# Memory and place of the turned even tiles between a first attention and a long convolution

## The chip, the cores and the metric

The kernel runs on one core of one Trainium2 chip. The metric is the device time of one execution in microseconds (us), the median of several runs. In the profile PE is TensorE, DVE is VectorE, ACT is ScalarE, POOL is GpSimd, and SP is SyncE, whose queue (SPq) issues nearly all transfers. An engine executes its instructions in the order in which they stand in its queue; an instruction that waits holds everything behind it on that engine.

## The reference

Two decoder layers are applied to a token matrix of 8 batches of 256 tokens with 512 features, in float32. After each of the six parts the result is added to the input and layer-normed.

```python
x = _layernorm(x + _L0_attn_ref(x, ...))            # differential attention, causal
x = _layernorm(x + _L0_xattn_ref(x, k, fside, ctx_2048, ctx_2048, 8))   # long convolution
x = _layernorm(x + _L0_ffn_ref(x, ...))             # 8 experts, two for each token
x = _layernorm(x + _L1_attn_ref(x, ...))            # causal attention
x = _layernorm(x + _L1_xattn_ref(x, ..., ctx_2048, ctx_2048, ...))      # cross attention
x = _layernorm(x + _L1_ffn_ref(x, ...))             # causal attention, one shared head by token
```

This case is about the border between the first two. The convolution takes the attended tokens and the context, forms their products kv for each group of 8 channels, filters kv along the features with a filter from `k`, and multiplies by the context again:

```python
kv = vr[:, :, :, None, :] * x2r[:, :, None, :, :]
y = irfft(rfft(kv, n=1024) * rfft(k, n=1024))[..., :512]
out = einsum('bhijl,bhil->bhjl', y + kv * skip, x1r)
```

Here the token position is the channel and the features are the axis that is filtered, so both inputs are needed turned: features on partitions, tokens on the free axis.

## The kernel before, in words

**Tiles.** The tokens lie in 16 tiles `x[t]` of 128 tokens by 512 features (NT = 16; t even is the first half of a batch, t odd the second). A turned tile is made by four PE transposes into PSUM and one copy out: `turned` (L227, copy on ACT at L232) inside an attention, `transpose` (L167, PE at L171) elsewhere, whose `evacuate` alternates the copy between ACT (L121) and DVE (L123).

**The first attention** (`diff_attention`, L291, through `causal_attention`, L1225) runs 64 units, 8 for each batch, in an order that is written out by hand for PE, DVE, ACT and POOL. A unit makes scores for row maxima (`maxima`, L1287), and nine units later the scores again as weights (`weights`: PE L1350 and L1359, exponential on ACT L1367, causal mask on POOL L1368) and the products with the values and with ones (`products`: PE L1393 and L1403, reciprocal on DVE L1411). Side work is put between these steps by `fill`, which spends a budget on each unit: first the steps of a list `after`, in order of the unit for which they were entered by `at(slots, "fill", ...)`, then a queue with due units. Side work of the last units: the output products (`ps_o`, PE L207), sums of squares and their powers (PE L514, L527, L553 with POOL L543 for the last batch but one; PE L450, L465 with POOL L458 and ACT L459 for the last batch, where each pair of units is scaled by itself), residuals and norms (DVE L267, L150, L151, L160, POOL L145, L146).

**The context.** From unit 54 on, one context tile is turned each unit (`turn_context`, PE L231, ACT L232) into a small buffer `cT`, and stored turned in DRAM as `ctx_d` (SP L429); it is loaded two tiles ahead (`load_context`, SP L424).

**The convolution** (`long_conv`, L571) works on two halves, i = 0 for the even tiles and i = 1 for the odd ones. `xh[i]` are turned tokens and `ch[i]` the turned context of a half. It loads `ch[0]` and `ch[1]` from `ctx_d` (SP L587), turns the even tiles into `xh[0]`, and then runs 32 groups h, the first 16 on half 0. A group loads its filter tile `wt` (SP L601, three buffers), makes kv on DVE and POOL (L607), side products u on POOL (L615, L616) with a sum `us` on DVE (L623), runs ten matmuls `ps_y` (PE L177, each two records in the trace) and multiplies and sums their results on DVE (L642, L645). The odd tiles are written down inside groups 0 and 1, and group 2 issues the loads of the experts' weights `gu` (SP L714, three of 2,816 KB). Their order on each engine is decided by the scheduler.

**Memory.** The four turned halves lie in two tiles of 32 KB a partition: `first` (`first_h`) holds `xh[0]` and `ch[0]`, `w` (`w_l1a`) holds `xh[1]` and `ch[1]`. In the built program `w` lies at bytes 196,576 to 229,344 of a partition, which nothing of the first attention uses, and `first` at 163,808 to 196,576, over the attention's buffers for residuals, wide rows, context and `cT` (its work memory ends at 196,256). A tile that is put over older ones waits for their last use. Later `w` takes the weights of the second layer's self attention; `first` takes the last part of the experts' weights, and after it is given back, `w_x` (`w_l1x`, a tile of the same size, elsewhere) takes the experts' gathered rows (`combine`, L1193) and the weights of the cross attention.

Of the kernel before, what the change touches and what calls it, by code (L numbers as in the profile page):

```python
# [17 lines left out]
F32 = mybir.dt.float32  # L18
# [6 lines left out]
P = 128  # L25
B, S, D = 8, 256, 512
NT = B * S // P
# [3 lines left out]
KB = D // P  # L31
# [14 lines left out]
PH = NT // 2  # L46
NE = (PH * 2 * P - E * (P - 1) - 1) // P + 1
VB = 64
NV = (NT - TPG) * P // VB + H1


@with_exitstack
def decoder_kernel(ctx: ExitStack, tc: tile.TileContext, a: dict, out: bass.AP):
    nc = tc.nc
    xin = a["x"].rearrange("b s d -> (b s) d").rearrange("(t p) d -> p t d", p=P)
    cin = a["ctx_2048"].rearrange("b s d -> (b s) d").rearrange("(t p) d -> p t d", p=P)
# [9 lines left out]
    x = []  # L66
# [134 lines left out]
    MM, TR = 0.86, 0.45  # L201
# [25 lines left out]
    def turned(pools, dst, src, tag="mm"):  # L227

        pt = pools.tile([P, KB, P], F32, tag=tag, name="pt")
        for k in range(KB):  # L230
            nc.tensor.transpose(pt[:, k, :], src[:, k * P : (k + 1) * P], ident)  # L231
        nc.scalar.copy(dst, pt)  # L232
# [55 lines left out]

    def diff_attention():  # L291

# [5 lines left out]
        w = wpool.tile([P, 7168], F32, tag="w", name="w_l0")  # L298
# [5 lines left out]
        for t in range(4):  # L304
            nc.sync.dma_start(
                out=wo[32 * t : 32 * t + 32],
                in_=a["L0_attn_Wo"][P * t : P * (t + 1), :].rearrange("(k d) c -> d k c", d=32),
# [5 lines left out]
        for i, n in enumerate(("q1", "k1", "q2", "k2")):  # L313
            nc.sync.dma_start(
                out=lv[:, i, :],
                in_=a[f"L0_attn_lambda_{n}"].unsqueeze(0).broadcast_to([P, HD0]),
# [13 lines left out]
        half = const.tile([P, 2], F32, tag="half", name="half")  # L330
# [25 lines left out]
        def prepare(work, pools, g, at, here):  # L356
            qT = work.tile([P, KB, GT], F32, tag="qT", name="qT")
            kz = work.tile([P, 2, GT], F32, tag="kz", name="kz")
            v = work.tile([P, TPG, P], F32, tag="v", name="v", bufs=3)
            xT, turns = turned_group(work, pools, g)  # L360
            batches = [slice(b * S, (b + 1) * S) for b in range(2)]

            def values(ti, ps=[]):
                if ti == 0:
                    ps.append(pools.tile([P, TPG, P], F32, tag="mm", name="ps_v"))
                for k in range(KB):
                    by_columns(
                        ps[-1][:, ti, :],
                        xT[0][:, k, ti * P : (ti + 1) * P],
                        wv[:, k, :],  # L370
                        k == 0,
                        k == KB - 1,
                    )
# [18 lines left out]

            if g:

                need = turns + [(0, values_steps), (0, keys(slice(0, GT)))]
            else:
                need = turns[:2] + [(0, keys(batches[0]))]
                need += [(3, steps) for _, steps in turns[2:]]
                need += [(8, keys(batches[1])), (9, values_steps)]
            for b, tokens in enumerate(batches):  # L400
                for c, first in enumerate((0, 1, 4, 5)):
                    block = feature_block(pools, qT, xT, wq, 0, c, HD0**-0.5, tokens)
                    need.append((8 * b + first, block))
            need.sort(key=lambda piece: piece[0])

            if g == NG - 1:

                for t in range(2):
                    load_context(work, t)
                for t in range(NT):  # L410
                    slot = 16 * g + 6 + t
                    at(slot - here, "fill", [(TR, lambda t=t: turn_context(work, pools, t))])
            return (
                need,
                lambda rows, c, at, n: qT[rows, c // 4 * 2 + c % 2, at : at + n],
                lambda rows, c, at, n: kz[rows, c // 2 % 2, at : at + n],
                lambda k, h: v[:, k, 32 * (h % 4) : 32 * (h % 4) + 32],
            )

        cx = {}  # L420

        def load_context(work, t):
            cx[t] = work.tile([P, D], F32, tag="cx", name="cx")
            nc.sync.dma_start(out=cx[t], in_=cin[:, t, :])  # L424

        def turn_context(work, pools, t):
            c = work.tile([P, KB, P], F32, tag="cT", name="cT")
            turned(pools, c, cx.pop(t))
            nc.sync.dma_start(out=ctx_d[:, :, t * P : (t + 1) * P], in_=c)  # L429
            if t + 2 < NT:  # L430
                load_context(work, t + 2)

        def gather(work, pools, at, yT, n, c, o, r):

# [136 lines left out]
    def long_conv(router, load_experts, xh, ch, ps_t, meanwhile):  # L571
# [5 lines left out]
        with ExitStack() as st:  # L577
# [4 lines left out]
            sk = work.tile([P, S], F32, tag="skip", name="skip", bufs=1)  # L582
            nc.sync.dma_start(out=sk, in_=skip.unsqueeze(0).broadcast_to([P, S]))
            tokens = ctx_d.rearrange("p k (b i s) -> p k b i s", b=B, i=2)
            for i in range(2):
                for k in range(KB):
                    nc.sync.dma_start(out=ch[i][:, k], in_=tokens[:, k, :, i, :])  # L587

            def turn(t):
                transpose(ps_t, xh[t % 2][:, :, t // 2, :], x[t])  # L590

            for t in range(0, NT, 2):
                turn(t)
            route = router(work)
            shape = [P, B, NHEAD, NHEAD]
            for h in range(NH):
                i, at = divmod(h * NHEAD, P)
# [979 lines left out]
    def self_weights(w, behind):  # L1577
        return load_w(w, 0, a["L1_attn_w_qkv"], 3 * D, behind), load_w(
            w, 3 * D * KB, a["L1_attn_w_o"], D, behind
        )  # L1580

    def self_attention(wqkv, wo, arrive):


# [76 lines left out]
    def cross_weights(w):  # L1661
        return [
            load_w(w, i * D * KB, a[f"L1_xattn_{n}"], D)
            for i, n in enumerate(("wq", "wk", "wv", "wo"))
        ]
# [519 lines left out]
        causal_attention("r", prepare, finish)  # L2185

    masks, clear_slots, load_experts, load_gu_last, router, blocks, combine, wide = experts(rt)
    diff_attention()
    with ExitStack() as st_self:


        half = B * P * KB
        pool = st_self.enter_context(
            tc.tile_pool(name="w_self", bufs=1, side="right", reuse_waits="tile")
        )
        w = pool.tile([P, 2 * half], F32, tag="w", name="w_l1a")
        with ExitStack() as st_blocks:
            pool = st_blocks.enter_context(
                tc.tile_pool(name="c_half", bufs=1, side="right", reuse_waits="tile")
            )  # L2200
            first = pool.tile([P, 2 * half], F32, tag="first", name="first_h")
            ps_t = st_blocks.enter_context(tc.tile_pool(name="c_pst", bufs=2, space=PSUM))
            parts = [
                [m[:, i * half : (i + 1) * half].rearrange("p (k b s) -> p k b s", k=KB, b=B) for m in (first, w)]
                for i in range(2)
            ]
            ends = [first[:, i * half : (i + 1) * half] for i in range(2)]
            late_tokens = long_conv(
                lambda work: router(work, w[:, half:]),
                load_experts,  # L2210
                parts[0],
                parts[1],
                ps_t,
                lambda: load_gu_last(ends),
            )
            w_self = []
            blocks(
                ps_t,
                [m[:, E * FF + i * D : E * FF + (i + 1) * D] for m in ends for i in range(2)],
                late_tokens,  # L2220
                lambda behind: w_self.extend(self_weights(w, behind)),
            )
        wide.close()
        x[:] = x_tiles(ctx.enter_context(tc.tile_pool(name="xb", bufs=1)))
        st_cross = ExitStack()
        pool = st_cross.enter_context(tc.tile_pool(name="w_cross", bufs=1))
        w_x = pool.tile([P, 8192], F32, tag="w", name="w_l1x")
        w_cross = []

        def arrive(t):  # L2230
            load, add, norm = combine(t, w_x)

            def last():
                norm()
                if t == NT - 1:
                    w_cross.extend(cross_weights(w_x))

            return load, add, last

        self_attention(*w_self, arrive)  # L2240
    with tc.tile_pool(name="w_routed", bufs=1, side="right") as pool:
        w_routed = routed_weights(pool.tile([P, 6400], F32, tag="w", name="w_l1f"))
        cross_attention(*w_cross)
        st_cross.close()
        routed_attention(*w_routed)
# [55 lines left out]
```

## Time and profile before

| | |
|---|---|
| time, median of 3 runs | 2091.62 us (2087.61 to 2092.78) |
| the profiled execution: its time and its span | 2084.03 us, 2082.3 us |
| what lies around the span | 1.7 us |
| mean granted clock of TensorE | 0.979 |
| busy: PE, DVE, POOL, ACT | 1926.0, 1236.9, 851.9, 615.3 us |
| last norm of the first attention (DVE L160, starts) | 465.57 us |
| first convolution matmul (`ps_y`, starts) | 476.4 us |
| last convolution matmul (starts) | 774.0 us |

The span is one execution from the first instruction to the last, and all positions below are in us from its start. The profiled execution was 7.6 us faster than the median of the runs, so its durations are used for differences, and a difference is then added to the median. PE's busy time counts modelled ends of pipelined matmuls. Rows of the timeline merge instructions of one line that follow each other; "idle before" names what the engine waited for.

### The profile page before, as it was taken

The numbers are of one execution on the slowest core, as the hardware profiler recorded it, in microseconds if no ns is written. First come the engines' busy times: TensorE is split into PE (matmuls) and PEld (weight loads), VectorE is DVE, ScalarE is ACT, GpSimd is POOL, SyncE is SP. The second block draws the span as 40 slices with busy tenths as digits, with TensorE's granted clock in tenths as the row PEclk, the third lists the DMA queues.
The fourth block names the chain that finished last, engine by engine and source line by source line (L and its number), as shares of the span: only waits on it lengthen the run. The fifth ranks groups of instructions, "written<-read, shape, count | busy, mean of one in ns | idle before, by whom it ended". The sixth has DMA issues, their size and how long they took to land. (4 is left out here: it accounts for less than half of the span.)

```text
span 2082.3 us, 46237 instructions
## 1 busy us (share of the span) xinstructions
PE 1926.0 (92%) x20068; PEld 1122.6 (54%) x20068; DVE 1236.9 (59%) x1879; ACT 615.3 (30%) x787; POOL 851.9 (41%) x945
## 2 busy tenths in 40 slices
PE   7979999879999999999969999998999999988985
PEld 5545555444444446666635545544878778454443
DVE  4677777658889876122225657457343442536887
ACT  4555555520000003211114344431101011235552
POOL 2677777646555834000014545344000000216763
PEclk9999999989999999999989999999999999999997
DMA  6799943326114217223122202002000000170000
GB/s 220 307 399 387 386 139 78 88 69 224 44 58 140 80 51 233 85 72 138 61 86 83 78 31 89 3 2 103 21 21 31 21 31 1 43 233 12 30 24 31
DMA packets 141627, 220.27 MB, mean 106 GB/s; under 512 B 27440, under 2 KB 56240, under 8 KB 141424
## 3 DMA queue, kind: packets, MB, share of 16 engines
q1 hardware_dynamic: 134960, 196.97, 27.5%
q0 software_dynamic: 6464, 20.32, 2.9%
q8 instruction: 160, 2.62, 0.5%
q14 instruction: 43, 0.35, 0.1%
HBM read 106.51 MB, written 123.34 MB: 110 GB/s over the span
## 5 line engine op out<-in xcount | busy, mean ns | idle before, releaser
L1411 DVE RECIPROCAL rsum<-ps_pv 128x256 f32<-128x256 f32 x128 | 224.5, 1754 | 220.2 <-PE ps_pv L1403 220.2
L177 PE MATMUL ps_y<-kv,wt 128*128 128x512 f32 x640 | 280.2, 597 | 5.4 <-POOL kv L607 2.7
L1367 ACT ACTIVATE pT<-ps_k 128x1536 f32<-128x1536 f32 x128 | 185.7, 1451 | 239.1 <-PE ps_k L1359 233.5
L1307 DVE TENSOR_REDUCE neg<-rows 128x12 f32<-128x1536 f32 x128 | 222.9, 1742 | 48.2 <-POOL rows L1298 48.1
L1296 ACT COPY rows<-ps_q 128x1536 f32<-128x1536 f32 x128 | 184.1, 1438 | 154.2 <-PE ps_q L1287 101.1
L1368 POOL TENSOR_SCALAR_AFFINE_SELECT pT<-pT 128x1024 f32<-128x1024 f32 x128 | 140.7, 1100 | 186.2 <-ACT pT L1367 186.1
L177 PEld LDWEIGHTS ps_y<-kv,wt 128*128 128x128 f32 x640 | 120.9, 191 | 156.7 <-issue 137.4
L1298 POOL TENSOR_SCALAR_AFFINE_SELECT rows<-rows 128x1024 f32<-128x1024 f32 x128 | 141.2, 1103 | 154.0 <-ACT rows L1296 153.4
L1378 POOL TENSOR_TENSOR pT<-pT 128x512 f32<-128x512 f32 x112 | 147.1, 1313 | 9.3
L1204 POOL DMA_INDIRECT w_l1x<-ys,slots x32 | 33.5, 1046 | 258.5 <-DMA ys<-y_m 250.9
L207 PE MATMUL ps_f<-xT,w_l1a 128*32 128x256 f32 x2048 | 122.0, 384 | 0.7 <-ACT xT L232 0.7
L145 POOL TENSOR_SCALAR rstd<-bn_mv 128x1 f32<-128x1 f32 x80 | 16.6, 207 | 206.8 <-DVE bn_mv L151 200.5
L1112 PE MATMUL po_m<-dn,hT 128*128 (+1 forms) x216 | 98.7, 594 | 1.0 <-ACT hT L1102 1.0
L1403 PE MATMUL ps_pv<-pT,ones_v 128*32 128x256 f32 (+1 forms) x1152 | 85.2, 378 | 14.7 <-POOL pT L1378 14.6
L645 DVE TENSOR_REDUCE yc<-z 128x64 f32<-128x512 f32 x128 | 86.2, 674 | 5.6 <-POOL w_l1a L646 5.2
L207 PEld LDWEIGHTS ps_f<-xT,w_l1a 128*32 128x32 f32 x2048 | 62.2, 111 | 45.3 <-issue 7.3
L1287 PE MATMUL ps_q<-kz,qT 32*128 32x128 f32 x1536 | 62.2, 292 | 16.8 <-ACT pT L1367 13.4
L1287 PEld LDWEIGHTS ps_q<-kT,qT 32*128 32x128 f32 x1536 | 48.7, 186 | 50.4 <-ACT pT L1367 17.3
L1350 PE MATMUL ps_k<-qT,kT 32*128 32x256 f32 (+1 forms) x1024 | 69.8, 359 | 5.1 <-ACT rows L1296 2.9
L1287 PEld LDWEIGHTS ps_q<-kz,qT 32*128 32x128 f32 x1536 | 49.8, 190 | 45.4 <-ACT pT L1367 31.8
L1091 DVE TENSOR_TENSOR h_b<-h_b,pg 128x352 f32<-128x352 f32 x36 | 18.8, 521 | 92.4 <-ACT h_b L1090 92.4
L1287 PE MATMUL ps_q<-kT,qT 32*128 32x128 f32 x1536 | 61.0, 288 | 13.4 <-ACT pT L1367 8.5
(385 smaller groups left out, 3617.4 us busy)
## 6 DMA issues: line engine op xcount, KB each, us to landing
xs<-zero SPq DMA_DIRECT2D x8, 4352.0 KB, 32.5
ys<-zero SPq DMA_DIRECT2D x8, 4352.0 KB, 33.1
filters<-in_L_xattn_k SPq DMA_DIRECT2D x4, 2560.0 KB
first_h<-xs SPq DMA_DIRECT2D x36, 256.0 KB, 2.7
ys<-y_m SPq DMA_DIRECT2D x36, 256.0 KB, 2.0
gu<-in_L_ffn_gate_up_proj SPq DMA_DIRECT2D x3, 2816.0 KB, 16.4
wt<-filters SPq DMA_DIRECT2D x32, 256.0 KB, 2.6
sorted_x<-zero SPq DMA_DIRECT2D x1, 5120.0 KB, 34.7
```

The lines of the kernel that those rows point to most:

```text
L177: nc.tensor.matmul(ps, lhsT=lhsT(k), rhs=rhs(k), start=(k == 0), stop=(k == n - 1))
L207: nc.tensor.matmul(ps[cs], lhsT=lhsT[:, cs], rhs=rhs, start=start, stop=stop)
L645: nc.vector.tensor_reduce(yc[:, lb], z, AX.X, ALU.add)
L1112: nc.tensor.matmul(po, lhsT=hT[:m, i, :], rhs=dn[i][:m, bass.ds(e, 1), :], start=(i == 0), stop=(i == len(FCH) - 1),)
L1287: nc.tensor.matmul(block[:, s, j, :], lhsT=q(rows, c, b * S + i * P, P), rhs=k(rows, c, b * S + keys * P, P), start=True, stop=True,)
L1296: nc.scalar.copy(d.rearrange("p j s k -> p s j k"), block)
L1298: nc.gpsimd.affine_select(out=rows, in_=rows, compare_op=ALU.is_ge, fill=-FAR, base=0, pattern=[[0, 8], [-1, P]], channel_multiplier=1,)
L1307: return lambda: nc.vector.tensor_reduce(neg[u // upb % 2][:, :, :, c], d, AX.X, ALU.max, negate=True)
L1367: nc.scalar.activation(p[:, 0:3].rearrange("p j s q -> p s j q"), block, AF.Exp)
L1368: nc.gpsimd.affine_select(out=p[:, 0:2].rearrange("p j s q -> p (j s) q"), in_=p[:, 0:2].rearrange("p j s q -> p (j s) q"), compare_op=ALU ...
L1378: nc.gpsimd.tensor_tensor(p[:, 3], p[:, 1], p[:, 2], ALU.add)
L1411: nc.vector.reciprocal(r, ps[:, 1, :])
```

## The change

`first` is now allocated before the first attention, at the outer end of the right side of the memory, and kept until the cross attention is done. In the built program it lies where `w` was (196,576 to 229,344), and `w` now lies over the attention's buffers (163,808 to 196,576). `diff_attention` gets the two halves of `first`:

- Context tiles are taken in the order 0, 2, ..., 14, 1, 3, ..., 15. The even ones are turned directly into `ch[0]`, and stored from there; the odd ones go through `cT` as before. So `long_conv` loads `ch[1]` alone.
- Six steps `turn_first` (EARLY = 6) turn the tiles x[0], x[2], ..., x[10] into `xh[0]`, entered at units 62 to 67. `long_conv` turns only x[12] and x[14] of the even tiles.
- `first` also takes the place of `w_x`, and the weights of the last part go to the left side of the memory.

In the built program the instructions of the attention's last units are ordered anew, since six steps more pass through `fill`. At the start of the convolution PE has the remaining turns, all eight odd ones included, and the four small matmuls `ps_cs` of the routing ahead of the first `ps_y`; SP has `skip`, the four loads of `ch[1]`, three filter tiles, the three loads of `gu`, and then the other filter tiles (before: `ch[1]`, `skip`, `ch[0]`, five filter tiles, `gu`). After that the order on every engine is the old one, but for a memset that moves by two instructions.

```diff
+EARLY = B - 2
-    def diff_attention():
+    def diff_attention(xh, ch):
...
-                for t in range(NT):
-                    slot = 16 * g + 6 + t
-                    at(slot - here, "fill", [(TR, lambda t=t: turn_context(work, pools, t))])
+                for i in range(NT):
+                    slot = 16 * g + 6 + i
+                    at(slot - here, "fill", [(TR, lambda i=i: turn_context(work, pools, i))])
+                for b in range(EARLY):
+
+                    def turn_first(b=b):
+                        turned(pools, xh[:, :, b, :], x[2 * b])
+
+                    at(16 * g + 14 + b - here, "fill", [(TR, turn_first)])
...
+        order = [*range(0, NT, 2), *range(1, NT, 2)]
...
-        def turn_context(work, pools, t):
-            c = work.tile([P, KB, P], F32, tag="cT", name="cT")
-            turned(pools, c, cx.pop(t))
+        def turn_context(work, pools, i):
+            t = order[i]
+            if t % 2:
+                c = work.tile([P, KB, P], F32, tag="cT", name="cT")
+            else:
+                c = ch[:, :, t // 2, :]
+            turned(pools, c, cx.pop(i))
             nc.sync.dma_start(out=ctx_d[:, :, t * P : (t + 1) * P], in_=c)
...
-            for i in range(2):
-                for k in range(KB):
-                    nc.sync.dma_start(out=ch[i][:, k], in_=tokens[:, k, :, i, :])
+            for k in range(KB):
+                nc.sync.dma_start(out=ch[1][:, k], in_=tokens[:, k, :, 1, :])
...
-            for t in range(0, NT, 2):
+            for t in range(2 * EARLY, NT, 2):
                 turn(t)
...
-    diff_attention()
+    st_cross = ExitStack()
+    pool = st_cross.enter_context(tc.tile_pool(name="w_first", bufs=1, side="right"))
+    first = pool.tile([P, 2 * half], F32, tag="first", name="first_h")
...
+    diff_attention(in_batches(first, 0), in_batches(first, 1))
...
-            pool = st_blocks.enter_context(
-                tc.tile_pool(name="c_half", bufs=1, side="right", reuse_waits="tile")
-            )
-            first = pool.tile([P, 2 * half], F32, tag="first", name="first_h")
...
-        st_cross = ExitStack()
-        pool = st_cross.enter_context(tc.tile_pool(name="w_cross", bufs=1))
-        w_x = pool.tile([P, 8192], F32, tag="w", name="w_l1x")
...
-            load, add, norm = combine(t, w_x)
+            load, add, norm = combine(t, first)
...
-    with tc.tile_pool(name="w_routed", bufs=1, side="right") as pool:
+    with tc.tile_pool(name="w_routed", bufs=1) as pool:
```

More of the change, by code (lines that the diff above doesn't have):

```diff
@@ L406, in prepare @@
             if g == NG - 1:
-                for t in range(2):
-                    load_context(work, t)
-                for t in range(NT):
-                    slot = 16 * g + 6 + t
-                    at(slot - here, "fill", [(TR, lambda t=t: turn_context(work, pools, t))])
+                for i in range(2):
+                    load_context(work, i)
+                for i in range(NT):
[5 more added lines that the diff above has]
+                    at(16 * g + 14 + b - here, "fill", [(TR, turn_first)])
             return (
@@ L420, in diff_attention, with load_context @@
         cx = {}
-        def load_context(work, t):
-            cx[t] = work.tile([P, D], F32, tag="cx", name="cx")
-            nc.sync.dma_start(out=cx[t], in_=cin[:, t, :])
-        def turn_context(work, pools, t):
-            c = work.tile([P, KB, P], F32, tag="cT", name="cT")
-            turned(pools, c, cx.pop(t))
+        order = [*range(0, NT, 2), *range(1, NT, 2)]
+        def load_context(work, i):
+            cx[i] = work.tile([P, D], F32, tag="cx", name="cx")
+            nc.sync.dma_start(out=cx[i], in_=cin[:, order[i], :])
+        def turn_context(work, pools, i):
[5 more added lines that the diff above has]
+            turned(pools, c, cx.pop(i))
             nc.sync.dma_start(out=ctx_d[:, :, t * P : (t + 1) * P], in_=c)
-            if t + 2 < NT:
-                load_context(work, t + 2)
+            if i + 2 < NT:
+                load_context(work, i + 2)
         def gather(work, pools, at, yT, n, c, o, r):
@@ L2187, in decoder_kernel, with in_batches @@
     masks, clear_slots, load_experts, load_gu_last, router, blocks, combine, wide = experts(rt)
-    diff_attention()
+    half = B * P * KB
+    st_cross = ExitStack()
+    pool = st_cross.enter_context(tc.tile_pool(name="w_first", bufs=1, side="right"))
+    first = pool.tile([P, 2 * half], F32, tag="first", name="first_h")
+    def in_batches(m, i):
+        return m[:, i * half : (i + 1) * half].rearrange("p (k b s) -> p k b s", k=KB, b=B)
+    diff_attention(in_batches(first, 0), in_batches(first, 1))
     with ExitStack() as st_self:
-        half = B * P * KB
         pool = st_self.enter_context(
@@ L2197, in decoder_kernel @@
         with ExitStack() as st_blocks:
-            pool = st_blocks.enter_context(
-                tc.tile_pool(name="c_half", bufs=1, side="right", reuse_waits="tile")
-            )
-            first = pool.tile([P, 2 * half], F32, tag="first", name="first_h")
             ps_t = st_blocks.enter_context(tc.tile_pool(name="c_pst", bufs=2, space=PSUM))
[L2203 to L2206, printed above, removed]
+            parts = [[in_batches(m, i) for m in (first, w)] for i in range(2)]
             ends = [first[:, i * half : (i + 1) * half] for i in range(2)]
@@ L2235, in last @@
                 if t == NT - 1:
-                    w_cross.extend(cross_weights(w_x))
+                    w_cross.extend(cross_weights(first))
             return load, add, last
         self_attention(*w_self, arrive)
-    with tc.tile_pool(name="w_routed", bufs=1, side="right") as pool:
+    with tc.tile_pool(name="w_routed", bufs=1) as pool:
         w_routed = routed_weights(pool.tile([P, 6400], F32, tag="w", name="w_l1f"))
```

## The prediction

> **What bounds the kernel now.** First the page's busy times:
>
> ```profile
> PE 1926.0 (92%) x20068; PEld 1122.6 (54%) x20068; DVE 1236.9 (59%) x1879; ACT 615.3 (30%) x787; POOL 851.9 (41%) x945
> ```
>
> PE is the bound on average, so the places that matter are those where it idles. I looked at the border between attention and convolution, first in the timeline of PE (start, us, engine, line, operation, records; in brackets the idle time before and what ended it):
>
> ```profile
> 424.79 0.86 PE L1393 MATMUL ps_pv<-pT,v 128*32 128x256 f32 x16 [2.03 <-POOL pT L1368]
> ...
> 445.31 0.86 PE L1393 MATMUL ps_pv<-pT,v 128*32 128x256 f32 x16 [0.49 <-DVE res L267]
> ...
> 449.12 0.44 PE L465 MATMUL pt_rr<-ident,wide 128*128 128x128 f32 x2 [2.31 <-ACT wide L459]
> 449.49 5.36 PE L207 MATMUL ps_o<-w_l,yT_b 128*32 128x512 f32 x48
> ...
> 459.07 3.64 PE L207 MATMUL ps_o<-w_l,yT_b 128*32 128x512 f32 x16 [0.58 <-DVE yT_b L468]
> 466.91 5.86 PE L171 MATMUL pt<-ident,x 128*128 128x128 f32 x28 [4.20 <-ACT first_h L121]
> ...
> 476.44 4.13 PE L177 MATMUL ps_y<-kv,wt 128*128 128x512 f32 x9 [0.19 <-DMA wt<-filters]
> ```
>
> The last products start at 445.31; 4.20 us of idle stand before the turns, and `ps_y` starts at 476.44, released by a filter tile. The timeline of SP's queue says why that tile comes so late:
>
> ```profile
> 430.19 3.88 SPq L587 DMA_DIRECT2D w_l1a<-ctx_d  x4
> 440.84 0.35 SPq L583 DMA_DIRECT2D skip<-in_fside_S  x1
> 466.27 3.68 SPq L587 DMA_DIRECT2D first_h<-ctx_d  x4
> 470.00 24.22 SPq L601 DMA_DIRECT2D wt<-filters  x5
> 498.13 6.86 SPq L714 DMA_DIRECT2D gu<-in_L_ffn_gate_up_proj  x3
> ```
>
> The odd context (`w_l1a`) goes out at 430.19, during the attention. The even one waits until 466.27, and the filters stand behind it. In the timeline of DVE, what it waits for is the last norm of `x[15]`, whose input `res` lies under `first`; it ends at 465.57 + 0.55 = 466.12:
>
> ```profile
> 465.57 0.55 DVE L160 TENSOR_SCALAR x<-res,bn_mv,rstd 128x512 f32<-128x512 f32 x1 [0.72 <-POOL rstd L146]
> ```
>
> The border thus has four stretches: up to the last products, from there to the norm (445.31 to 466.12, 20.8 us), from the norm to the first `ps_y` (10.3 us), and the first groups.
>
> **The change part by part.** The profiled execution takes 2084.03 us (span 2082.3 and 1.7 around it); the median is 2091.62. Differences are made against the former and added to the latter.
>
> *Memory and queue.* `first` becomes free early, but `w` takes its place over `res`. The loads of `ch[1]`, 2 MB like those of `ch[0]`, now wait for the norm of `x[15]`, and they still stand ahead of the filters on SP. So the transfers from norm to first filter tile are the old ones: four context loads, then `wt`, 10.2 us. What the change takes off this path (loading `ch[0]`) it puts back as `ch[1]`.
>
> *A, last units of the attention.* Six turns enter. One turn costs PE 0.58, 0.49 and 0.58 us (from the start of an L231 row to the next row: 417.24 to 417.82, 426.23 to 426.72, 409.64 to 410.22): 6 × 0.55 = 3.3. Behind the last products move two of the turns L171 (1.04 together at 443.78), one L450 (0.47) and one L465 (0.25): −1.8. Net +1.5. The six copies on ACT (0.58 each) are hidden: ACT is busy some 6 to 14 us of 52 here, and nothing of PE waits for them soon; uncovered they would cost 3.5.
>
> The order also makes a new wait. In one late unit POOL now has, between two masks L1368, two L543 and one L458; PE's L465, which needs that L458 by way of ACT, stands ahead of the next unit's scores, and behind it are those scores, the weights and the products of the unit. The timeline of POOL has the prices:
>
> ```profile
> 420.43 3.26 POOL L543 TENSOR_TENSOR rr<-rr,neg_half 128x8 f32<-128x8 f32 x2
> 423.64 1.09 POOL L1368 TENSOR_SCALAR_AFFINE_SELECT pT<-pT 128x1024 f32<-128x1024 f32 x1
> 424.70 1.64 POOL L458 TENSOR_TENSOR rr<-rr,neg_half 128x8 f32<-128x8 f32 x1
> ```
>
> 3.26 + 1.64 = 4.9 us, of which one product step of PE (about 1.5, L1393 and L1403) lies beside: +3.4. Against it, waits of PE before (5.6 us between 403 and 445, among them the 2.03 shown at 424.79, and 1.97 at 412.83) partly go, since the turns fill them: −2. A = 1.5 + 3.4 − 2 = +3. Bounds: no new wait, and all that the turns can fill goes (1.5 − 3.3 = −1.8); the whole wait and nothing filled (+4.9). I take +3: the order fixes the new wait, and of the old ones I let one of about 2 us be filled.
>
> *B, last products to last norm.* The moved L450, L465 and the order of the `ps_o` blocks (24, 8 of the last batch's tiles) lengthen the steps before the 48 records, which I place 7.5 us after the products instead of 4.2; the wait of 2.42 us for ACT `wide` that stood later goes. Added up by the rows: 7.5 + 5.4 (48 records) + 0.8 (L465 and its DVE step) + 1.9 (16 records, by their row of 1.90 at 431.82) + 3.4 (462.71 to 466.12) = 19.1. Before, 20.8 with the last 16 records at 3.64 us instead of 1.90: the same 19.1 at full clock. Whether these records meet the half clock decides: −1.7 to +1.7, and I take 0.
>
> *C, norm to first `ps_y`, 10.3 before.* The filter comes at 10.2 as before. The other chain: one copy of `x[14]`'s turn 0.7, kv and u on POOL (1.06 + 1.17 + 1.06 + 0.72 + 0.72 = 4.7), `us` 0.4, two copies of odd turns 1.3 and three kv 2.2 on DVE, `us` 0.4, copy 0.7, the turn of `x[15]` 0.7 and the four `ps_cs` 0.95, which PE now has ahead of `ps_y`: 12.05. Being later, it decides: +1.7 (bounds −0.1, if the filter alone decides, to +3.3, if DVE's kv and POOL's do not overlap as well).
>
> *D, first groups.* Before, 100 records of `ps_y` take from 476.44 to 523.64, 47.2 us; at 0.438 each (five groups of 20 records, 8.76 each) they are 43.8. The 3.4 us are three odd turns, `ps_cs` and a wait of 1.84 us at 497.45, all of which now lie ahead of the first `ps_y`: −3.4 (bound 0, if `ps_y` waits for kv instead).
>
> *E, the clock.* Windows of 3.41 us (busy us and instructions of each engine, then granted clock, DMA share, GB/s):
>
> ```profile
> 457.47:460.88 3.41, 2.50 (x14) 0.78 (x18) 0.42 (x1) 0.28 (x1) 0.00 (x0) 0.50 0.00 0
> 460.88:464.29 3.41, 1.83 (x12) 0.10 (x4) 3.01 (x6) 0.00 (x0) 0.74 (x2) 0.50 0.00 0
> 464.29:467.70 3.41, 0.79 (x4) 0.79 (x5) 1.80 (x4) 0.58 (x1) 0.94 (x2) 0.50 0.06 11
> 467.70:471.12 3.42, 3.42 (x17) 2.84 (x16) 0.99 (x2) 1.17 (x2) 0.00 (x0) 0.50 1.12 299
> 471.12:474.53 3.41, 2.64 (x19) 1.76 (x17) 2.57 (x5) 1.56 (x3) 0.00 (x0) 1.00 1.19 291
> ```
>
> After a thin window those that follow run at half clock, and a full window brings the clock back. Now about nine turns (5 us of work) are spread over the 12 us to `ps_y`, 41% busy, so that the first 3.4 us of `ps_y` may run at half: one window's work done by half, +1.7 (0 to +3.4).
>
> The Trainium skill ("TensorE: Matmul & The Clock Gate", Part 4) speaks against such a stretch: it says that PE's transposes are not counted as busy and do not bring the full clock. The rows differ: from 467.70 to 471.12 PE had turns alone, and 1.00 follows. By the rule the first window of `ps_y` is at half clock whatever the turns' density; by the row only if they are sparse.
>
> *Later stages.* The orders are the old ones. The even context is no longer loaded, and the loads of odd context move where they were. The cross attention's context is ready some 30 us before it is used; its new waits hide there. I cost them at nothing; uncovered, one wait shifts by 3 us at most.
>
> *Sum.* 3 + 0 + 1.7 − 3.4 + 1.7 = +3.0: 2087.0 us for an execution like the profiled one, 2094.6 for the median. A measurement can tell 0.3%, 6.3 us, from no change.
>
> **The rivals.** *(1) The forecast: next to nothing, −3 to +6.* A load is exchanged for a load, and six turns of PE work change place.
>
> *(2) Faster.* If the norm no longer gates the filter (SP past the context sooner), or the even group's kv is ready at once, `ps_y` starts 7 us earlier: with A at its lower end and D, 2091.6 − 7 − 1.8 ≈ 2083 at best. For it: 4.20 us of PE idle at 466.91, 10.35 us of POOL waiting for `first_h` at 475.88. Against it: SP's order keeps 2 MB behind the norm and ahead of `wt`.
>
> *(3) Slower: the clock.* If the half clock outlasts the first window of `ps_y`, each further window costs 1.7 on top of +3. With two more, 3 + 3.4 = +6.4: 2098; with three, 2099.7. It decides from two. For it: the four half windows above; against it: `ps_y` once running is dense, and one full window sufficed.
>
> *(4) Slower: the filter behind `gu`.* The fourth `wt` now stands behind three loads of 2,816 KB. Before, these went out at 498.13 and had landed at about 521.4, 23.3 us later. Now they go out about 12.5 us after the norm, while the fourth filter is needed 26.3 us after the first `ps_y` (three groups of 8.76), which is itself at 12. Margin about 3 us. At the rate of the context loads in the windows above (299 GB/s) they take 28.8 us: PE then stalls for about 5 us, +8 in all: 2099.6. It decides from a `gu` time of about 26 us. For it: SP's order and the rate beside the context; against it: the measured 23.3.
>
> **How the numbers follow.** (1) has 0.6, of which little reaches below or beyond the bound; (2) 0.10; (3) 0.10; (4) 0.20. So faster 0.10; slower takes (3), (4) and the upper end of (1), 0.37; same 0.53. The range goes from 2086.4, A's lower end with D and no loss in C and E (−1.8 − 3.4), to 2101.5, (4) with A at its upper end (+8 + 1.9).
>
> **What would show it.** The first `ps_y` 11 to 13 us after the norm of `x[15]`, `ch[1]`'s loads on SPq right after that norm, `wt` after them; an idle of about 3 us of PE before an L465 in the last units; no odd turn between `ps_y`; one window at 0.50 after the first `ps_y`. Wrong would be: `ps_y` less than 8 us after the norm (rival 2), several windows at 0.50 (3), a wait of `ps_y` for `wt` some 26 us on (4), or any difference after 530 us above 3 us, which my reading of the order excludes.

## The result, and the profile after

The changed kernel takes 2093.83 us (median of 17 runs, 2088.22 to 2100.48); the kernel before, in 17 runs beside them, 2089.76 us (2086.07 to 2095.51). The ratio is 1.0023, interval 1.0012 to 1.0034: 2.5 to 7 us slower. Forecast were 2094.6 us, and +3. A second set of runs on one chip, with both kernels profiled again (c1 and c2 below), gave the same ratio.

The profiled execution spans 2092.1 us. In the page, PE's busy time has grown by 8 us with the same number of instructions:

```profile
PE 1934.2 (92%) x20068; PEld 1126.7 (54%) x20068; DVE 1236.1 (59%) x1876; ACT 617.4 (30%) x790; POOL 851.2 (41%) x945
```

Same work, more time: PE ran more of it at half clock (the granted clock in the trace is 0.50 for 104.5 us in all, 87.5 before). Of the 9.8 us between the two spans, 6.5 were there already at 376 us, ahead of the first instruction that the change puts in another place: some windows of 3.41 us at half clock that one execution has and the other not. Two spans are therefore no measure of this change. I set a mark at the start of a product for row maxima (`ps_q`) shortly ahead of the first moved instruction, 376.36 in the kernel before and 382.90 in the changed one, and compare stretches from there.

In the timeline of PE of the changed kernel (lines have moved: `ps_y` is now L178, the turns L172, L465 is L478):

```profile
435.67 0.44 PE L478 MATMUL pt_rr<-ident,wide 128*128 128x128 f32 x2 [3.19 <-ACT cT L233]
...
452.88 0.83 PE L1405 MATMUL ps_pv<-pT,v 128*32 128x256 f32 x16
...
460.69 6.92 PE L208 MATMUL ps_o<-w_l,yT_b 128*32 128x512 f32 x48
...
473.36 1.27 PE L172 MATMUL pt<-ident,x 128*128 128x128 f32 x8 [2.87 <-DVE x L161]
...
482.03 2.90 PE L172 MATMUL pt<-ident,x 128*128 128x128 f32 x12 [3.04 <-DVE w_l1a L124]
...
486.52 1.88 PE L178 MATMUL ps_cs<-rw,ones_m 128*128 128x8 f32 x8
488.26 57.07 PE L178 MATMUL ps_y<-kv,wt 128*128 128x512 f32 x129
```

The forecast wait stands at L478 (3.19 us; what it hangs on is shown further down). The norm of `x[15]` ends at 474.57 and `ps_y` starts 13.7 us later, but not on a filter: a turn before it waits 3.04 us for a copy on DVE. No odd turn stands between the first 129 records of `ps_y`. SP's queue is as foreseen, with the odd context right behind the norm and the filters behind it:

```profile
449.06 0.33 SPq L596 DMA_DIRECT2D skip<-in_fside_S  x1
474.70 3.74 SPq L599 DMA_DIRECT2D w_l1a<-ctx_d  x4
478.48 2.69 SPq L613 DMA_DIRECT2D wt<-filters  x3
486.75 6.26 SPq L726 DMA_DIRECT2D gu<-in_L_ffn_gate_up_proj  x3
```

DVE says why the copies come late:

```profile
474.02 0.55 DVE L161 TENSOR_SCALAR x<-res,bn_mv,rstd 128x512 f32<-128x512 f32 x1 [0.72 <-POOL rstd L147]
474.49 0.68 DVE L124 COPY first_h<-pt 128x512 f32<-128x512 f32 x1
475.20 3.29 DVE L619 TENSOR_TENSOR kv<-first_h 128x512 f32<-128x512 f32 x3
480.81 0.42 DVE L635 TENSOR_REDUCE us<-u 128x32 f32<-128x256 f32 x1 [2.31 <-POOL u L628]
481.28 1.29 DVE L124 COPY w_l1a<-pt 128x512 f32<-128x512 f32 x2
482.48 3.06 DVE L619 TENSOR_TENSOR kv<-first_h 128x512 f32<-128x512 f32 x3
```

Since the early half is complete one copy after the norm, kv of two groups starts at once, on DVE and on POOL. The copies of the odd turns (481.28) stand behind three kv and behind a sum that waits 2.31 us for POOL; the turns on PE stand behind the copies, and `ps_y` behind the turns. The windows from the norm on (busy us of PE, PEld, DVE, ACT, POOL, clock, DMA share, GB/s) are all at half clock until `ps_y` has filled one; in those ahead of it PE is busy for 33% to 80% of the time:

```profile
477.58:481.00 3.42, 1.12 (x4) 0.72 (x4) 1.11 (x2) 0.23 (x1) 3.42 (x5) 0.50 1.20 299
481.00:484.40 3.40, 2.37 (x11) 2.15 (x12) 3.35 (x6) 0.59 (x1) 3.40 (x5) 0.50 1.16 317
484.40:487.80 3.40, 2.72 (x13) 2.12 (x12) 3.09 (x6) 0.59 (x1) 2.44 (x4) 0.50 0.28 101
487.80:491.26 3.46, 3.46 (x7) 1.91 (x8) 1.37 (x4) 0.00 (x0) 3.30 (x6) 0.51 0.91 309
```

### The profile page after: what moved, and what is told of

Read it like the earlier page. It is cut to its first block, busy times and chain, and to the rows that moved or that the text cites. A ratio compares the mean times of both kernels' runs of the same rounds, so it can differ in the third digit from the quotient of the medians.

```text
span 2092.1 us, 46235 instructions
## 1 busy us (share of the span) xinstructions
PE 1934.2 (92%) x20068; PEld 1126.7 (54%) x20068; DVE 1236.1 (59%) x1876; ACT 617.4 (30%) x790; POOL 851.2 (41%) x945
## 5 line engine op out<-in xcount | busy, mean ns | idle before, releaser
L178 PE MATMUL ps_y<-kv,wt 128*128 128x512 f32 x640 | 281.0, 599 | 5.3 <-POOL kv L619 2.7
L178 PEld LDWEIGHTS ps_y<-kv,wt 128*128 128x128 f32 x640 | 121.7, 192 | 158.7 <-issue 139.2
L1216 POOL DMA_INDIRECT first_h<-ys,slots x32 | 33.5, 1046 | 258.2 <-DMA ys<-y_m 250.6
L1415 PE MATMUL ps_pv<-pT,ones_v 128*32 128x256 f32 (+1 forms) x1152 | 86.2, 381 | 14.0 <-POOL pT L1390 13.8
```

What stands on the lines that cost most here:

```text
L178: nc.tensor.matmul(ps, lhsT=lhsT(k), rhs=rhs(k), start=(k == 0), stop=(k == n - 1))
L1415: nc.tensor.matmul(ps[32 * s : 32 * s + 32, 1, j * P :], lhsT=ones_v, rhs=p[:, 1, s, :] if j else first[:, :, s, :], start=(j == 0), stop= ...
```

## The experiments

The theory: what the change takes off the start of the convolution is put back by the odd turns ahead of `ps_y` and by SP's order, and the list's turns cost a little in the attention's last units. The rivals: turns cost their 0.55 us wherever they stand; the filter's landing alone sets the start; part of the cost lies in later stages. One table carries all runs, in us. *A* goes from the mark to the last products, *B* to the end of the norm of `x[15]`, *C* to the first `ps_y`, *D* over its first 300 records, and the total goes to the last one (the records after the first 300 take 163.3 to 165.7 in all runs and are not listed), with the ratio of each to the kernel before on its own chip (the kernel before took 2089 to 2100 us on these chips).

| run | A | B | C | D | total | ratio (95%) |
|---|---|---|---|---|---|---|
| before | 68.95 | 20.81 | 10.32 | 133.12 | 397.60 | 1 |
| c1 before again | 66.61 | 20.80 | 10.35 | 133.12 | 395.29 | 1.0007 (0.9996 to 1.0018) |
| changed | 69.98 | 21.69 | 13.69 | 130.29 | 399.99 | 1.0023 (1.0012 to 1.0034) |
| c2 changed again | 70.06 | 21.73 | 13.67 | 130.32 | 400.11 | 1.0023 (1.0012 to 1.0035) |
| e1 no early turns | 68.71 | 22.09 | 12.94 | 128.83 | 396.91 | 1.0028 (1.0018 to 1.0039) |
| e2 filters first | 70.48 | 21.96 | 4.21 | 134.18 | 395.22 | 1.0012 (0.9998 to 1.0026) |
| e3 copies on ACT | 70.47 | 22.00 | 10.50 | 130.33 | 397.68 | 1.0004 (0.9993 to 1.0014) |
| e4 turns sooner | 68.31 | 20.40 | 13.69 | 131.86 | 399.98 | 1.0006 (0.9996 to 1.0016) |
| e5 = e1 + e2 | 68.83 | 22.50 | 4.21 | 134.24 | 394.11 | 0.9995 (0.9982 to 1.0008) |
| e6 = e2, odd later | 70.44 | 21.94 | 4.21 | 132.61 | 392.49 | 0.9989 (0.9975 to 1.0002) |
| e7 = e5, odd later | 69.71 | 22.47 | 4.21 | 132.58 | 392.27 | 0.9973 (0.9958 to 0.9989) |
| e8 = e7, copies on ACT | 70.18 | 21.72 | 3.49 | 131.11 | 390.90 | 0.9981 (0.9963 to 0.9998) |
| e9 = e2, weights later | 70.89 | 21.51 | 4.21 | 134.17 | 394.98 | 1.0001 (0.9986 to 1.0017) |
| e10 before, filters first | 68.37 | 20.82 | 7.69 | 134.15 | 394.36 | 0.9991 (0.9976 to 1.0005) |

B, C and D repeat within 0.05 us between the two profiles of each of the two kernels. A does not: half-clock windows come and go in it. Before has two that c1 lacks, 2.3 us in all: one at the mark, which both profiles of the changed kernel have too, and one 37 us behind it.

**c1 and c2, the two kernels again.**

> The kernel before, unchanged, profiled on the chip of this call as a measure for the others. Theory (the change touches nothing after the last ps_y): the time from there to the end is the same as in the changed kernel of this call, within 3 us, which is two windows at half clock; ratio 1.000. Rival (a part of the change's cost lies later, in the experts or the second layer): it is shorter here by more than 3 us.

> The changed kernel, unchanged, on the same chip. Theory (all of the change's cost lies between the last batch's row maxima and the last ps_y): that stretch is 2 to 3 us longer than in the kernel before of this call, and the ratio 1.001 to 1.002. Rival (part of it lies later): the stretch is 2 to 3 us longer and the rest too by over 3 us; ratio above 1.003.

The stretch is 4.8 us longer in c2 than in c1 (2.4 in the first pair, where the kernel before had its two windows). From the last `ps_y` to the end it is 1311.93 and 1312.35 us. So on this chip nothing of the cost lies later, and the ratio's 4.8 us are all in the stretch. That is what both theories say of the place of the cost. Its size was missed in c2: 4.8 us instead of 2 to 3, and a ratio of 1.0023 instead of 1.001 to 1.002. A part of the 4.8 is the window at the mark, which c1 lacks.

**e1, no early turns.** `EARLY = B - 2` becomes `EARLY = 0`.

> The memory move and the direct turning of the even context stay; no token tile is turned by the list of the last units (EARLY = 0), all eight even turns are left to the convolution's code and the scheduler sets seven of them between the last products and the last norm; the order of the tail is then that of the kernel before. Theory (the list's turns lengthen the last units by their work and by a new wait behind POOL, and PE's waits after the last products could have held them): the stretch up to the last products shrinks by about 1 us against the changed kernel, to 69.0; the stretch from there to the norm is 21 to 22 (seven turns, 3.9 us, mostly in waits); norm to the first ps_y stays 13 to 14, since the odd turns stand ahead of it; about 2092 to 2093, or 1 us under the changed kernel. Rival (a turn costs PE its 0.55 us wherever it stands): the stretch to the norm grows by 3.9 and the kernel is 2 to 3 us slower than the changed one.

The stretches came as the theory has them (A 68.7, with one half-clock window 27 us after the mark; B 22.1; C 12.9), and the total is 3.1 us under the changed kernel. Of the seven even turns, three came to stand at the end of A and four in B. The rival's growth of B by 3.9 is not there: B has three turns more than in the changed kernel, 1.7 us at 0.55 each, and grew by 0.4, so most of their work lies in waits. But the measured ratio, 1.0028, does not follow its stretch. After the last `ps_y` its profile has 1319.2 us, 7 to 10 more than in c1 and the changed kernel; at the first experts PE waits 2.9 us for a copy on ACT, which none of the traces of c1, c2, before and after has. e2 to e4, on the same chip, and e7 to e10, on a third, show 1315 to 1324 there as well, and the kernel before was slower on these chips by 6 and 10 us. All eight of these traces have a stall of ACT (5.1 to 7.3 us, for which they name no instruction) 53 to 57 us after the last `ps_y`; the six from the other chips, e5 and e6 among them, have none. e10 is the kernel before with three loads moved, and it has the stall too (5.85 us on ACT, 3.75 on PE). So the stall goes with the chip and not with the change, and if the kernel before has it on e1's chip too, it does not explain e1's ratio. The profiled execution of e1, 2096.95 us, was the fastest of its nine and 4.8 under their median, so what made the others slower is in no trace: e1's ratio stays open.

**e2, filters first.**

```diff
+            wts = []
+            for h in range(3):
+                wt = work.tile([P, D], F32, tag="wt", name="wt", bufs=3)
+                nc.sync.dma_start(out=wt, in_=toeplitz(h))
+                wts.append(wt)
             tokens = ctx_d.rearrange("p k (b i s) -> p k b i s", b=B, i=2)
...
-                wt = work.tile([P, D], F32, tag="wt", name="wt", bufs=3)
-                nc.sync.dma_start(out=wt, in_=toeplitz(h))
+                if h < 3:
+                    wt = wts[h]
...
```

> As the changed kernel, but the loads of the first three filter tiles stand ahead of the four loads of odd context on SP; the scheduler then sets four turns ahead of the first ps_y and six of the rest behind it. Theory (SP's 2 MB of odd context, and the order that follows from it, set the start of ps_y): from the norm to the first ps_y 5 to 7 us instead of 13.7, the first 300 records longer by 4 to 5 us for the turns between them; net 3 to 4 us faster than the changed kernel, 2089 to 2091, about level with the kernel before. Rival (ps_y waits for kv on DVE and POOL, not for the filter): norm to ps_y stays over 10 us and the time within 1 us of the changed kernel.

In its timelines of SP and PE:

```profile
446.35 2.31 SPq L600 DMA_DIRECT2D wt<-filters  x3
471.89 3.82 SPq L604 DMA_DIRECT2D w_l1a<-ctx_d  x4
```

```profile
475.96 18.56 PE L178 MATMUL ps_y<-kv,wt 128*128 128x512 f32 x40
```

The filters now go out during the attention, 25 us ahead of the context, and `ps_y` starts 4.2 us after the norm, 9.5 sooner. D is longer by 3.9 for the turns and `ps_cs` that moved between the records, and the total 4.8 shorter. The theory holds (4.2 is even below its 5 to 7); the gain of time, 2 us by the two ratios, which come from different chips, is less clear than that of the stretch.

**e3, copies on ACT.** In the convolution's `turn`, `transpose(...)` becomes `turned(...)`, whose copy is on ACT.

> As the changed kernel, with all copies of the turns at the convolution's start on ACT instead of alternating between ACT and DVE; the order on PE and SP is untouched. Theory (the odd turns ahead of ps_y wait for their copies on DVE, which stand behind kv and behind a sum that waits for POOL): the wait of 3.04 us of PE for DVE is gone, norm to ps_y 10.5 to 11.5 instead of 13.7, then the filter (10.2) is next; 2 to 3 us faster than the changed kernel, 2091 to 2092. Rival (the filter's landing sets the start, and the turns only fill the time until then): norm to ps_y stays at 13 to 14 and the time at 2094.

```profile
470.96 5.57 PE L232 MATMUL pt<-ident,x 128*128 128x128 f32 x28 [0.24 <-ACT first_h L233]
476.51 1.06 PE L178 MATMUL ps_cs<-rw,ones_m 128*128 128x8 f32 x8
481.34 3.89 PE L178 MATMUL ps_y<-kv,wt 128*128 128x512 f32 x5 [3.77 <-DMA wt<-filters]
```

The wait for DVE is gone and seven turns run in a row; C is 10.5, and now the filter is what `ps_y` waits for, 3.77 us. That settles the order of the two limits in the changed kernel: the copies on DVE at 13.7, the filter 3.2 us below them.

**e4, turns six units sooner.** `16 * g + 14 + b` becomes `16 * g + 8 + b`; some of these tiles are then turned before their norm, so the convolution reads them as they were ahead of it.

> As the changed kernel, but the six early turns are entered six units sooner, so that the tail has the order of the kernel before and no L478 stands ahead of its POOL power. Theory (about half of what the change costs up to the last products is that new wait, the rest the turns' own work): the wait of 3.19 us at L478 is gone, waits of about 2 us that the kernel before had come back, the turns cost 3.3 us in units where PE is dense; up to the last products +2 to +3 against the kernel before (changed kernel: +1.0), to the norm 20.8 as before (-0.9); 2093 to 2095. Rival (the new wait is what the change costs there, the turns are filled in): up to the last products 69 or less, and 2 us faster than the changed kernel.

The wait at L478 is gone. A is 68.3, 1.7 under the changed kernel and 1.7 over c1, and B is 20.4. But A no longer holds the turns: five of the six now lie 2 to 31 us ahead of the mark, and A has as many turns as in the kernel before. Its 1.7 us over c1 go with a half-clock window 27 us behind the mark, which c1 lacks. The price of the turns is to be read ahead of the mark: the 37.5 us there take 0.1 us longer than in c1, and PE's idle time in them is 2.3 us less. So five turns, about 2.7 us of work, went into waits nearly for nothing, and the rival was right in that the turns are filled in. Its 2 us did not come in the total, 399.98, which is that of the changed kernel (the ratio, 1.0006, is from another chip). What A and B gain, D (+1.6) and the records after it (+1.4) lose to half-clock windows: 6.1 us of `ps_y` run at half clock at its start instead of 2.95, and later two windows instead of one.

All six profiles that have the list's late turns and that wait (changed, c2, e2, e3, e6, e9) have a half-clock window 54 to 55 us after the mark, just behind the wait; the eight without have none there.

**e5, e6, e9: adding up.** e5 joins e1 and e2. e6 is e2 with the odd turns over four groups and the weights issued in group 4; e9 is e2 with the weights alone:

```diff
-                if h < 2:
-                    for t in range(h * PH + 1, (h + 1) * PH, 2):
+                if h < 4:
+                    for t in (4 * h + 1, 4 * h + 3):
                         turn(t)
-                    if h == 1:
+                    if h == 3:
                         x_first.close()
```

> The memory move and the direct turning of the even context; no tile turned early by the list; the first three filter tiles loaded ahead of the odd context. PE has seven even turns between the last products and the norm, then five turns, then ps_y, and four odd turns and ps_cs between the first ps_y. Theory (start-up is set by SP's 2 MB and the odd turns ahead of ps_y; the list's turns cost about 1 us): up to the norm about 90.8 as without the early turns, norm to ps_y 4 to 6, and the stretch from the row maxima to the last ps_y 393 to 395, 3 to 5 us under the kernel before; ratio 0.998 to 0.999. Rival (the two do not add, since the turns that the list made would have to stand ahead of ps_y): the stretch is 396 to 398.

> As the changed kernel with the first three filter tiles ahead of the odd context, and the odd turns written down two a group in the first four groups (before: four in the first two), the experts' weights then issued in group 4 instead of 2. Theory (turns between ps_y cost their 0.55 us and the waits for their copies, wherever they stand once ps_y runs): the stretch from the row maxima to the last ps_y is that of filters first, 395, within 1 us. Rival (the weights of the experts and the filters behind them crowd the first groups): it is 2 us or more shorter.

> As filters first, with the experts' weights in group 4 instead of 2 in the program; on the queue their place is the same as in filters first. Theory (the 1.6 us by which the spread odd turns shorten the first 300 records come from the turns' waits, 1.33 us at one of them, not from the weights): the first 300 records take 134 as in filters first (134.2). Rival (the weights crowd the filters): 132.6 as with the spread turns.

e5: 394.1, as the sum of its parts had it; its ratio, 0.9995, is a little over what I expected. e6 was a miss: D is 1.6 us shorter than in e2, where I expected the same. The rival of e6, that the weights crowd the filters, was to be settled by e9, where D stays at 134.17. But e9 moves the weights in the program alone: on SP's queue they stand behind two more filters as in e2, and only in e6 behind four. In the timelines of SP of e2, e9 and e6, in this order:

```profile
499.57 6.49 SPq L734 DMA_DIRECT2D gu<-in_L_ffn_gate_up_proj  x3
501.60 6.56 SPq L734 DMA_DIRECT2D gu<-in_L_ffn_gate_up_proj  x3
512.98 7.44 SPq L734 DMA_DIRECT2D gu<-in_L_ffn_gate_up_proj  x3
```

What speaks against the rival is e2's trace: in its first 300 records PE waits once, 1.33 us, for a turn's copy on DVE, and never for a filter; e6 has no wait there. So 1.3 of the 1.6 us are that wait.

**e7 and e8, the parts together.**

> The memory move and the direct turning of the even context, no tile turned early by the list, the first three filter tiles ahead of the odd context, the odd turns two a group in the first four groups and the experts' weights in group 4. Theory (the gains of the parts add: 1.1 us without the early turns, 1.6 for the odd turns' waits): the stretch from the row maxima to the last ps_y is 391 to 393, 3 to 5 us under the kernel before (395.3); ratio 0.998 to 0.9985. Rival (seven turns between the last products and the norm and the later odd turns meet the half clock): 393 to 395, ratio 0.999 to 1.000.

> As the combined version, with all copies of the convolution's turns on ACT. Theory (PE's waits for copies on DVE before and between the first ps_y, 0.7 to 0.8 us each, go): norm to ps_y 3 to 4 instead of 4.2, the stretch 1 us shorter than in the combined version, ratio about 0.998. Rival (ACT alone takes longer for a row of copies, 0.59 us each with two buffers, and five turns ahead of ps_y instead of four): norm to ps_y 4.5 to 5.5, no gain.

Totals of 392.3 and 390.9 us, 3 and 4.4 under c1, and ratios of 0.9973 and 0.9981, both clear of 1 and not apart from each other: 4 to 6 us faster than the kernel before, and 9 to 10 faster than the changed one, by the ratios. B in e7 and e8 carries four of the seven even turns at 0.9 to 1.7 us over c1; e8's expected gain of 1 us in the stretch is there (C 3.5, D 1.5 less), not in its ratio.

**e10, the filters alone.** The edit of e2 in the kernel before.

> The kernel before with only its first three filter tiles moved ahead of the even context on SP: nothing of the change. Theory (the even context itself, which this kernel loads after the norm, is then what ps_y waits for by way of kv): norm to first ps_y 9.5 to 11 as before (10.3), ratio 1.000 within 0.1%; the change's direct turning is what lets ps_y start at 4.2. Rival (the filter tile alone sets the start): norm to ps_y under 8, and the stretch from row maxima to the last ps_y 2 us or more shorter than in the kernel before.

```profile
478.33 1.07 POOL L615 TENSOR_TENSOR kv<-first_h 128x512 f32<-128x512 f32 x1 [10.26 <-DMA first_h<-ctx_d]
```

C is 7.7, not 9.5 to 11: the theory fell in part, and the rival's "under 8" came, though not its 2 us in the total (0.9 under c1). With the filter there, `ps_y` starts on the first blocks of the context, while the last (POOL's kv) still waits 10.26 us for its landing. D loses 1.0 again. So the filters' place is worth 1.6 us in C and D without the change, and 5.6 with it (e2 against the changed kernel): `ps_y` starts at 4.2 only with the even context in place too.

## Why the prediction was right

- **Memory and queue** held: one 2 MB load replaced another behind the norm, and the filter lands 10.5 us after it (e3). It was not the last to arrive, as step C said.
- **A**, forecast +3: +1.0 in the first pair, +3.4 in the second; the kernel before's windows, which it has in one run and not in the other, make the difference. With the window at the mark on both sides and none other of chance it is +2.2 to +2.3 in either pair (an estimate: each of the two windows of before taken at half of their 2.3 us). The new wait was forecast at 3.4 and is 3.19, by the instructions named. In the timelines of POOL and ACT:

```profile
429.85 3.23 POOL L556 TENSOR_TENSOR rr<-rr,neg_half 128x8 f32<-128x8 f32 x2
433.05 1.64 POOL L471 TENSOR_TENSOR rr<-rr,neg_half 128x8 f32<-128x8 f32 x1
434.72 0.40 ACT L472 COPY wide<-rr 128x256 f32<-128x256 f32 x1 [3.32 <-POOL rr L471]
435.03 0.58 ACT L233 COPY cT<-pt 128x512 f32<-128x512 f32 x1
```

  L478 starts at 435.67, as soon as the second of these copies on ACT is done, and that one stands behind the copy that waits for POOL. Two parts of A were off against each other: nearly all of the new wait is made up by old waits that went (PE's waits from the mark to the last products sum to 8.8 us in c1 and 8.1 in c2; I let 2 of 3.4 go), and the half-clock window behind the wait was not in the sum: the steps from 436.03 to 440.12 take 4.1 us, the same steps from 442.90 to 445.26 at full clock 2.4.
- **B**, forecast 0: +0.9. The 16 records run at full clock as assumed (1.92 us), but the half clock moved to the 48 records, 6.92 instead of 5.36.
- **C**, forecast +1.7, measured +3.4, just over its upper bound. The chain was the right one up to its end: the turn of `x[15]` (0.7) runs beside the last copy on DVE and not behind it, and PE's last turns, at half clock, are through at the same moment as that copy (486.5), so two paths meet at `ps_cs`. Three terms were too small by about 0.9 each: three kv beside POOL took 3.06 instead of 2.2, POOL's two kv 1.5 each instead of 1.06, and `ps_cs` 1.88 instead of 0.95 at half clock. e3, where no copy of these turns is on DVE, shows that these copies are the limit.
- **D and E**, forecast −3.4 and +1.7, together −1.7: measured −2.8, with one window of `ps_y` at half clock inside, as forecast.
- **Sum**: +3.0 forecast, +2.4 and +4.8 in the stretch of the two pairs, +4.1 in the medians. So the mechanism was right, and the closeness is partly luck: C was 1.7 us over its forecast, D and E together 1.1 under it, and in the first pair A was 2 under it. That the time came within 0.8 us of the forecast 2094.6 is luck too: the base was the median of three runs, 2091.62, and the median of seventeen is 2089.76.
- **Rivals.** (2) is what e2 and e5 to e8 build: it needs another SP order, and then `ps_y` starts at 3.5 to 4.2 us. (3) did not come: one window. (4) did not come: PE never waits for `wt` in the changed kernel's first groups.
- **Rule and row.** The Trainium skill ("TensorE: Matmul & The Clock Gate", Part 4) would have kept the clock down through the turns. e3 measures it: in the window 470.77 to 474.18 PE has turns alone, at 0.51, and the next is at full clock:

```profile
470.77:474.18 3.41, 3.22 (x15) 2.86 (x16) 3.31 (x5) 2.17 (x5) 3.19 (x3) 0.51 0.54 156
474.18:477.60 3.42, 3.30 (x23) 2.31 (x21) 2.12 (x4) 2.66 (x5) 3.42 (x4) 1.00 1.20 295
```

  Here the row decides: a window full of turns brings the clock back. In the changed kernel the turns were too thin for that (33% to 80% busy in the rows further up).

## What to carry to other kernels

When a buffer is moved so that one load becomes free early, look at what takes the old place and stands in the same queue: here the second context half inherited the wait, and the filters stood behind it as before. Work that was hidden in one wait (the odd turns behind a running `ps_y`) can come to stand ahead of the first critical instruction, and its copies behind new work on another engine; moving the load that does not depend on the late norm ahead (e2), leaving fill work to the waits that are there anyway (e1), and spreading the odd turns (e6) made of the same program one that is 0.2 to 0.3% faster than the kernel before (e7, e8). How much of that is due to the memory move is not shown: the kernel before with the filters ahead alone (e10) has a total of 394.4 us and a ratio of 0.9991, the memory move with the filters ahead and no early turns (e5) 394.1 and 0.9995, and the odd turns were not spread without the move.

## What the runs showed of the hardware

- kv on DVE takes 0.68 us alone (473.65 in the kernel before) and 1.02 to 1.10 on average in the two rows of three of the changed kernel, where POOL has its own kv, u and r; POOL's kv takes 1.5 us there and 1.06 at the same place of the kernel before (475.88 and 478.04). DVE's copies out of PSUM stay at 0.68 to 0.69 beside POOL's work. The Trainium skill ("GPSIMD Engine Reference", 1. Specifications) says that GpSimd shares its SBUF interfaces with VectorE and that they contend when DVE has two SBUF inputs; the rows agree.
- A single wait of 3.2 us of PE amid dense work was followed by one window at half clock in every one of the six profiles that have it (in the changed kernel the clock is 0.57 from 436.1 to 439.5, and the products in that window, L1405 and L1415, take 1.51 and 1.45 us instead of 0.86 and 0.83).
- The same program (the kernel before) took 2089, 2096 and 2100 us on three chips; a difference of 0.2% is only read from runs beside each other. On the two slower chips every trace has a stall of ACT of 5.1 to 7.3 us at the first experts, and no trace from elsewhere has it.
